# Two of the four pairs of row tiles: weights times values as seven half-size products

## The chip, the cores and the metric

The kernel runs on one core of a Trainium2 chip. The time is device microseconds of that core for one launch; shorter is better. Several runs are taken and their median is compared. One further execution is recorded by the hardware profiler; its own time and its span are given below.

## The reference

Eight sequences (batches) of 1024 rows by 256 columns, float32, go through one block: a modulated layer norm, attention without projections (both score sides are the normed rows times a vector), a gated residual, a second modulated norm, a two-layer ReLU network of inner width 1024 with a gated residual.

```python
h = layernorm(x) * (1 + ca) + sa
scores = einsum('nsd,ntd->nst', h * w_lhs, h * w_rhs)
x = x + ga * einsum('nst,ntd->nsd', softmax(scores), h)
h = layernorm(x) * (1 + cb) + sb
x = x + gb * (relu(h @ W1 + b1) @ W2 + b2)
```

`ca`, `sa`, `ga`, `cb`, `sb`, `gb` come from a small product per sequence; the gates are kept at least 0.25 away from zero. Everything stays float32. The change concerns the second `einsum`: weights times values.

## The kernel before

A batch has 1024 rows, that is eight row tiles of 128. One pass of the main loop is called a turn here: turn `i` of batch `b` handles row tile `i` of that batch. The instructions of each engine stand in the order in which the program names them (`pin` fixes that), so every engine works through one list and an instruction that waits holds up all behind it on its engine.

In a turn the kernel computes the scores of the tile two turns ahead (`direct`, L381: only blocks on or right of the diagonal; `psc` in PSUM, copied to `sc` by ScalarE), mirrors the rest (`mirror`: VectorE transposes 32x32 blocks, DMAs issued by SyncE put them in place), takes the maximum of each row (`row_max`, L431, VectorE, tile `m`), spreads that maximum along the columns with a small transposing matmul (`max_turn`, L436, `pm`), subtracts it (`subtract`, L443, VectorE) into the transposed weights `pT` (128 keys by 8 blocks by 128 rows), and exponentiates them in place (`exponent`, L452, ScalarE).

`product` (L464) then multiplies the tile's `pT` by the batch's values `xg`: eight matmuls, one for each block of 128 keys, of 257 columns (256 values and a column of ones, whose result is the sum of the row's weights), summed in one PSUM bank `po`. `product_out` takes the reciprocal of that sum (L478), scales and adds to `x` (L480) and takes the statistics of the new row for the second norm (L227, L228), all on VectorE. `ffn_stats`, `ffn_norm` and what follows need these statistics of four row tiles.

The network of the batch half before runs in the same turns. Batch `b`'s turns 0, 1, 4 and 5 hold its first layer: `pair_products` (L579) with `pair_sums` (L613 to L622), `pair_last` (L630 and, on GpSimd, L631), `pair_relu`, and `pair_turn` (L650 to L653, GpSimd). That layer already works by seven half-size products. Turns 2 and 3, 6 and 7 hold the second layer (`y_first` and `y_second`, L657, with their sums on VectorE and the transpose `y_turn`, L714). Next to this, the next batch is loaded, normed and transposed (`prepare_...`; its transposes are L305, its sides `lT` and `rT` are written at L335 and L339). Batch 0 has no network before it, and the last batch's network runs after the loop.

From batch 1 on, `product(b, i)` and `product_out(b, i)` stand at the end of each turn; only in turns 6 and 7 of the last batch do they stand at the start. `max_turn` stands between two matmuls of a turn's network part: in turns 0, 1, 4 and 5 behind the first two products of `pair_products`, in turns 2, 3, 6 and 7 inside `y_first` and `y_second`. The row maximum of tile 6 is taken on VectorE at the end of turn 4 and is wanted on TensorE early in turn 5; that of tile 7 is taken and wanted within turn 5. PSUM banks tagged `a` (four) hold `po`, `pa`, `pb`, `pc`, `ya` to `yd` in turn. Small GpSimd additions (`later`) wait in a list that `spare` takes from at fixed places.

Of the kernel before, what the change touches and what calls it, by code (L numbers as in the profile page):

```python
# [10 lines left out]
F32 = mybir.dt.float32  # L11
AF = mybir.ActivationFunctionType
ALU = mybir.AluOpType
# [3 lines left out]
P = 128  # L17
# [5 lines left out]
def adaln_block_kernel(  # L23
# [13 lines left out]
    nc = tc.nc  # L37
    B, S, D = x.shape
    INTER = W1.shape[1]
    NT = S // P  # L40
# [184 lines left out]
    def stats(mv, t, src, name):  # L225
        st = work.tile([P, nc.vector.BN_STATS_DIM], F32, tag="st", name=f"st_{name}")
        nc.vector.bn_stats(st, src)  # L227
        nc.vector.bn_aggr(mv[:, t, :], st)  # L228
# [90 lines left out]
    def prepare_turn(b, g, vector=True):  # L319

        xg, pts = xg_t[b], []
        lT = lT_t[b, g] = two.tile([P, ND, HALF], F32, tag="lT", name=f"lT_{b}_{g}", bufs=3)
        rT = rT_t[b, g] = two.tile([P, ND, HALF], F32, tag="rT", name=f"rT_{b}_{g}", bufs=3)
        rows = lambda T, k: T[:, k, :].rearrange("p (t a v) -> p t a v", a=NV, v=V)
        for k in range(ND):
            if b > 0:
                pt = pre[b, g][:, k]
            else:
                pt = ps_t.tile([P, HALF], F32, tag="t", name=f"pth_{b}_{g}_{k}")
                for j in range(TH):  # L330
                    nc.tensor.transpose(pt[:, ts(j, P)], xg[:, g * TH + j, ts(k, P)], ident)
                pt = pt.rearrange("p (t a v) -> p t a v", a=NV, v=V)
            pts.append(pt)
            if vector:
                nc.vector.tensor_scalar(  # L335
                    rows(lT, k), pt, side_col(0, 0, k, b), side_col(0, 1, k, b),
                    ALU.mult, ALU.add,
                )
            nc.scalar.activation(  # L339
                rows(rT, k), pt, AF.Identity,  # L340
                scale=side_col(1, 0, k, b), bias=side_col(1, 1, k, b),
            )
        if not vector:
            for k in range(ND):
                nc.scalar.activation(
                    rows(lT, k), pts[k], AF.Identity,
                    scale=side_col(0, 0, k, b), bias=side_col(0, 1, k, b),
                )
# [123 lines left out]
    def product_out(b, i):  # L472
        po = po_t.pop((b, i))
        g, j = divmod(i, TH)
        if j == 0:
            mvb_t[b, g] = work.tile([P, TH, 2], F32, tag="mvb", name=f"mvb_{b}_{g}")
        rl = work.tile([P, 1], F32, tag="rl", name=f"rl_{b}_{i}")
        nc.vector.reciprocal(rl, po[:, D : D + 1])  # L478
        x2 = x_tile(b, i)
        nc.vector.scalar_tensor_tensor(x2, po[:, :D], rl, x2, ALU.mult, ALU.add)  # L480
        stats(mvb_t[b, g], j, x2, f"b{b}_{i}")


    ffn = {}
# [5 lines left out]
    def spare():  # L490
        if queue:
            queue.popleft()()
# [4 lines left out]
    def ffn_stats(b, g):  # L497
        mv = mvb_t.pop((b, g))
        ffn["r", g] = mv, rstd_of(mv, "rb", f"rb_{b}_{g}")
# [269 lines left out]

    def second_out(b, a):  # L770
        q = a % 2
        if q == 0:
            out_t["o"] = work.tile([P, 2, D], F32, tag="o", name=f"o_{b}_{a}", bufs=2)
        o = out_t["o"]
        nc.vector.tensor_tensor(o[:, q, :], out_t.pop(a)[:, :D], x_tile(b, a), ALU.add)
        if a >= NT - 2:
            nc.sync.dma_start(out=out[b, ts(a, P), :], in_=o[:, q, :])
        elif q == 1:
            nc.sync.dma_start(
                out=out[b, ds((a - 1) * P, 2 * P), :].rearrange("(q p) d -> p q d", p=P),  # L780
                in_=o,
            )
# [209 lines left out]
    def weights(b, i):  # L992
        subtract(b, i)
        exponent(b, i)
# [3 lines left out]
    for b in range(B):  # L998
        for i in range(NT):
# [25 lines left out]
            if b == 0:  # L1025
# [20 lines left out]
                    subtract(*ahead)  # L1046
                norms(b, i)
                spare()
                continue
            turn_max = (lambda: max_turn(*late)) if late else (lambda: None)  # L1050

# [4 lines left out]
            if first:  # L1056
# [10 lines left out]
                if ahead:  # L1067
                    mirror(*ahead)
                pair_last(fb, fg, c)
                if c > 0:  # L1070
                    pair_turn(c - 1)
                if i == 4 and b + 1 < B:
# [8 lines left out]
                middle(b, i)  # L1081
                pair_sums(fb, fg, c + 1)
                pair_last(fb, fg, c + 1)
                if ahead and ahead != extra:
                    row_max(*ahead)
                pair_turn(c)
# [9 lines left out]
            else:  # L1096
                half = i % TH - 2
                if i == 3 and b + 1 < B:
                    prepare_stats(b + 1, 1)
                if not ahead:  # L1100

                    product(b, i)
                    product_out(b, i)
                    if i == NT - 1:
                        ffn_stats(b, 1)
                (y_second if half else y_first)(fb, fg, turn_max)
                if ahead:
                    mirror(*ahead)
                spare()
                early(b, i)  # L1110
                if late:
                    weights(*late)
                middle(b, i)
                if i == 2 and b + 1 < B:
# [19 lines left out]
            if not first:  # L1134
                if half and b < B - 1 or i == 3:
                    y_turn(fb, fg)
                for _ in range(4 if half else 1):
                    spare()
            if first or ahead:
                product(b, i)  # L1140
                product_out(b, i)
            if (b, i) == (B - 1, TH - 1):
                ffn_stats(b, 0)
            late = ahead if ahead != extra else None
# [86 lines left out]
```

## Time and profile before

| what | value |
|---|---|
| median of 3 runs | 778.18 us (778.14 to 778.81) |
| the profiled execution: its time, its span | 778.52 us, 776.6 us |
| granted TensorE clock | 1.00 |
| TensorE matmul busy | 767.0 us, 99% of the span |
| VectorE busy | 562.9 us, 72% |
| GpSimd busy | 461.5 us, 59% |
| ScalarE busy | 342.3 us, 44% |
| matmuls of weights times values (L464) | 1024 records, 233.0 us busy |

The page lists busy time for each engine, then groups of equal instructions with their number, total busy time, mean duration in ns and the idle time of the engine ahead of them. One float32 matmul of the program shows as two matmul records. Matmuls overlap, so a mean of 380 ns for one record is its latency; the time it takes from TensorE is the distance between two starts, which the timeline gives. The span leaves out what lies around the program's first and last instruction: 778.52 less 776.6, 1.9 us.

### The profile page before, as it was taken

The numbers are of one execution on the slowest core, as the hardware profiler recorded it, in microseconds if no ns is written. First come the engines' busy times: TensorE is split into PE (matmuls) and PEld (weight loads), VectorE is DVE, ScalarE is ACT, GpSimd is POOL, SyncE is SP. The second block draws the span as 40 slices with busy tenths as digits, with TensorE's granted clock in tenths as the row PEclk, the third lists the DMA queues.
The fourth block names the chain that finished last, engine by engine and source line by source line (L and its number), as shares of the span: only waits on it lengthen the run. The fifth ranks groups of instructions, "written<-read, shape, count | busy, mean of one in ns | idle before, by whom it ended". The sixth has DMA issues, their size and how long they took to land.

```text
span 776.6 us, 10553 instructions
## 1 busy us (share of the span) xinstructions
PE 767.0 (99%) x3374; PEld 619.7 (80%) x3374; DVE 562.9 (72%) x1212; ACT 342.3 (44%) x581; POOL 461.5 (59%) x573
## 2 busy tenths in 40 slices
PE   8999999999999999999999999999999999999998
PEld 3576788878887888878887888887888878888886
DVE  6597879658796688947788667966879667583632
ACT  4454545534354355434455344543535435251511
POOL 1365675936758386664857547594575927368641
PEclk9999999999999999999999999999999999999999
DMA  5314434355344364444443544445534345142220
GB/s 191 123 38 148 119 108 127 124 146 169 113 125 136 109 174 112 143 137 118 146 125 113 151 142 135 104 152 151 155 106 127 102 122 170 38 126 81 81 82 28
DMA packets 106208, 95.14 MB, mean 123 GB/s; under 512 B 29700, under 2 KB 98848, under 8 KB 106152
## 3 DMA queue, kind: packets, MB, share of 16 engines
q1 hardware_dynamic: 98408, 85.81, 37.7%
q10 hardware_dynamic: 7744, 8.65, 3.7%
q8 instruction: 27, 0.44, 0.2%
q14 instruction: 29, 0.24, 0.1%
HBM read 50.62 MB, written 43.81 MB: 122 GB/s over the span
## 4 chain that ended last, share of the span: by engine, by line
PE 88%; DVE 5%; POOL 2%; DMA 2%; issue 1%; ACT 1%; SPq 0%; DVEq 0%; POOLq 0%; ACTq 0%
PE po L464 26%; PE psc L381 15%; PE pa L579 9%; PE pb L579 6%; PE pc L579 6%; PE yc L657 6%; PE ya L657 6%; PE yb L657 6%; PE py L762 3%; PE yd L657 3%; PE pm L436 1%; POOL f L631 1%; DVE m L431 1%; DMA x<-in_L_attn_x_dram 1%; DMA D_y<-T_y 1%
## 5 line engine op out<-in xcount | busy, mean ns | idle before, releaser
L464 PE MATMUL po<-xg,pT 128*128 128x257 f32 x1024 | 233.0, 380 | 0.0
L464 PEld LDWEIGHTS po<-xg,pT 128*128 128x128 f32 x1024 | 193.9, 190 | 27.9 <-issue 1.0
L631 POOL TENSOR_TENSOR f<-f,kept 128x512 f32<-128x512 f32 x64 | 81.3, 1271 | 122.9 <-DVE f L630 104.6
L381 PE MATMUL psc<-rT,lT 128*128 128x512 f32 (+3 forms) x384 | 134.3, 486 | 0.0
L381 PEld LDWEIGHTS psc<-rT,lT 128*128 128x128 f32 x384 | 68.7, 190 | 38.7 <-issue 26.5
L388 ACT COPY sc<-psc 128x512 f32<-128x512 f32 (+3 forms) x96 | 45.0, 475 | 108.5 <-PE psc L381 108.5
L452 ACT ACTIVATE pT<-pT 128x1024 f32<-128x1024 f32 x64 | 67.1, 1048 | 50.3 <-DVE pT L443 50.2
L443 DVE TENSOR_TENSOR pT<-sc,pm 128x1024 f32<-128x1024 f32 x64 | 77.1, 1205 | 8.0 <-PE pm L436 8.0
L431 DVE TENSOR_REDUCE m<-sc 128x1 f32<-128x1024 f32 x64 | 77.3, 1209 | 0.1
L598 ACT COPY kept<-pa 128x512 f32<-128x512 f32 x64 | 37.4, 585 | 82.2 <-PE pa L579 82.2
L640 ACT ACTIVATE f<-f 128x512 f32<-128x512 f32 x64 | 40.4, 631 | 74.3 <-POOL f L631 74.3
L567 POOL TENSOR_TENSOR hs<-hT 128x256 f32<-128x256 f32 x16 | 11.6, 728 | 97.6 <-DVE hT L558 97.6
L579 PE MATMUL pb<-hs,w1s 128*128 128x256 f32 x256 | 66.0, 380 | 0.3 <-DVE f L616 0.3
L579 PE MATMUL pc<-hT,w 128*128 128x256 f32 x256 | 65.7, 379 | 0.0
L404 DVE STREAM_TRANSPOSE Tm<-sc 128x896 f32<-128x896 f32 (+6 forms) x49 | 34.7, 708 | 34.8 <-ACT sc L388 34.1
L579 PEld LDWEIGHTS pc<-hT,w 128*128 128x128 f32 x256 | 48.6, 190 | 6.6
L495 POOL TENSOR_TENSOR x<-x,rows 128x256 f32<-128x256 f32 x64 | 45.5, 739 | 12.1 <-ACT rows L865 12.1
L579 PEld LDWEIGHTS pb<-hs,w1s 128*128 128x128 f32 x256 | 45.9, 190 | 8.2 <-DVE f L616 0.8
L657 PE MATMUL yc<-f,w2s 128*128 128x256 f32 x224 | 52.1, 379 | 0.0
L613 DVE SCALAR_TENSOR_TENSOR u<-pb,cols,kept 128x256 f32<-128x256 f32 x64 | 30.5, 477 | 28.2 <-PE pb L579 27.2
L657 PEld LDWEIGHTS yc<-f,w2s 128*128 128x128 f32 x224 | 41.5, 190 | 10.2 <-issue 2.9
L651 POOL TENSOR_TENSOR ft<-ft,f 128x256 f32<-128x256 f32 x56 | 41.6, 744 | 4.4
(135 smaller groups left out, 1397.2 us busy)
## 6 DMA issues: line engine op xcount, KB each, us to landing
D_f<-T_f SPq DMA_DIRECT2D x60, 128.0 KB, 2.3
X_f<-D_f SPq DMA_DIRECT2D x15, 512.0 KB, 3.4
D_a<-T_a SPq DMA_DIRECT2D x56, 128.0 KB, 3.1
D_y<-T_y SPq DMA_DIRECT2D x56, 128.0 KB, 2.3
Y<-D_y SPq DMA_DIRECT2D x14, 512.0 KB, 4.0
out_dram<-x SPq DMA_DIRECT2D x14, 512.0 KB, 3.2
X_a<-D_a SPq DMA_DIRECT2D x13, 512.0 KB, 3.4
x<-in_L_attn_x_dram ACTq DMA_DIRECT2D x12, 512.0 KB, 3.4
```

The source lines that it names most:

```text
L381: nc.tensor.matmul(psc[:, : hi - lo], lhsT=lT_t[b, i // TH][:, k, ts(i % TH, P)], rhs=rT_t[b, n][:, k, lo - n * HALF : HALF], start=(k == ...
L388: nc.scalar.copy(score_row(b, i)[:, lo // V : hi // V, :], psc[:, : hi - lo].rearrange("p (n v) -> p n v", v=V),)
L431: nc.vector.tensor_reduce(m, score_row(b, i), AX.XY, ALU.max)
L443: nc.vector.tensor_tensor(pT.rearrange("p j (a v) -> p j a v", v=V), score_columns(b, i), pm[:, :P].rearrange("p (j a v) -> p j a v", j=1, ...
L452: nc.scalar.activation(pT_t[b, i], pT_t[b, i], AF.Exp)
L464: nc.tensor.matmul(po[:, : D + 1], lhsT=pT[:, t, :], rhs=xg_t[b][:, t, 0 : D + 1], start=(t == 0), stop=(t == NT - 1),)
L495: queue.append(lambda: nc.gpsimd.tensor_tensor(out, in0, row, op))
L579: nc.tensor.matmul(out, lhsT=lhsT, rhs=rhs, start=True, stop=True)
L631: nc.gpsimd.tensor_tensor(f[:, c::NH, hi], f[:, c::NH, hi], kept[:, None, hi].to_broadcast([P, 2, H2]), ALU.add,)
L640: nc.scalar.activation(f[:, c, :], f[:, c, :], AF.Relu)
L651: add(ft[:, 1, c], ft[:, 0, c], f[:, c, lo], ALU.add)
L657: nc.tensor.matmul(out, lhsT=lhs(c), rhs=rhs(c), start=(c == 0), stop=(c == NH - 1))
```

## The change

Row tiles 2 and 3, and row tiles 6 and 7, of batches 1 to 7 are taken together: fourteen pairs. For a pair, the weights (256 rows by 1024 keys) are a two by two block matrix: the two row tiles, and the two halves of the keys. The values are one too: the two halves of the keys, and the two halves of the columns, the second with the column of ones. Seven products of 128 rows by 512 keys by 128 or 129 columns (four matmuls each) take the place of eight.

`pair_begin` computes two of the seven, with the weights of the first tile as they are, at the start of turn 2 or 6. `left_sums` (GpSimd, four additions of 128x512) then forms the sums of the weights, partly in place in `pT`, and needs both tiles' exponentials. `right_sums` (GpSimd) forms the four sums of the values in `tsum`, once for a batch: three at the end of the turn 7 before, one in turn 0. `pair_end` computes the other five products at the end of turn 3 or 7, in two PSUM banks. `pair_begin_sum` and `pair_out` (VectorE) add the products up into `W` in SBUF. `pair_rows` does for both tiles what `product_out` did, from `W`. It stands in turn 4 behind the second `pair_last` and ahead of `row_max`; for tiles 6 and 7, and everywhere in the last batch, right after `pair_out`. In turn 2 `subtract` and `exponent` of tile 3 move ahead of `left_sums`. `max_turn` moves into `pair_begin` in turns 2 and 6.

`lT` and `rT` have two buffers in place of three, and the last batch's output tile lies in a buffer of the network (`ft`) as one piece of eight row tiles in place of two buffers of two.

```diff
@@ -319,8 +319,8 @@
     def prepare_turn(b, g, vector=True):
         xg, pts = xg_t[b], []
-        lT = lT_t[b, g] = two.tile([P, ND, HALF], F32, tag="lT", name=f"lT_{b}_{g}", bufs=3)
-        rT = rT_t[b, g] = two.tile([P, ND, HALF], F32, tag="rT", name=f"rT_{b}_{g}", bufs=3)
+        lT = lT_t[b, g] = two.tile([P, ND, HALF], F32, tag="lT", name=f"lT_{b}_{g}", bufs=2)
+        rT = rT_t[b, g] = two.tile([P, ND, HALF], F32, tag="rT", name=f"rT_{b}_{g}", bufs=2)
         rows = lambda T, k: T[:, k, :].rearrange("p (t a v) -> p t a v", a=NV, v=V)
         for k in range(ND):
             if b > 0:
@@ -479,6 +479,110 @@
         x2 = x_tile(b, i)
         nc.vector.scalar_tensor_tensor(x2, po[:, :D], rl, x2, ALU.mult, ALU.add)
         stats(mvb_t[b, g], j, x2, f"b{b}_{i}")
+    XS = D - P + 1
+    tsum = const.tile([P, 4, TH, P + 4], F32, name="tsum")
+    nc.gpsimd.memset(tsum[:, 1, :, P : P + 1], 1.0)
+    paired = lambda b, i: b > 0 and i % TH >= 2
+    def right_sums(b, which):
+        xg = xg_t[b]
+        b11, b12 = xg[:, 0:TH, P:D], xg[:, 0:TH, 0:P]
+        b21, b22 = xg[:, TH:NT, P:D], xg[:, TH:NT, 0:P]
+        t = [tsum[:, n, :, 0:P] for n in range(4)]
+        ins = [(b12, b11), (b22, t[0]), (b22, b12), (t[1], b21)]
+        for n in which:
+            nc.gpsimd.tensor_tensor(t[n], *ins[n], ALU.subtract)
+    halves = lambda pT: (pT[:, 0:TH, :], pT[:, TH:NT, :])
+    two_t = {}
+    def pair_begin(b, i, between=None):
+        W = work.tile([P, 2, D + 4], F32, tag="W", name=f"W_{b}_{i}", bufs=1)
+        pp = ps_a.tile([P, HALF], F32, tag="a", name=f"pp_{b}_{i}")
+        one, other = halves(pT_t[b, i])
+        rows = slice(P, P + XS)
+        for out, lhs, h in (
+            (pp[:, 0:XS], one, 0), (pp[:, XS : 2 * XS], other, 1)
+        ):
+            for t in range(TH):
+                nc.tensor.matmul(
+                    out, lhsT=lhs[:, t, :], rhs=xg_t[b][:, h * TH + t, P : P + XS],
+                    start=(t == 0), stop=(t == TH - 1),
+                )
+            if between and h == 0:
+                between()
+        nc.scalar.copy(W[:, 1, rows], pp[:, 0:XS])
+        two_t[b, i] = W, pp
+    def pair_begin_sum(b, i):
+        W, pp = two_t[b, i]
+        rows = slice(P, P + XS)
+        nc.vector.tensor_tensor(W[:, 0, rows], pp[:, XS : 2 * XS], W[:, 1, rows], ALU.add)
+    def left_sums(b, i):
+        (a11, a12), (a21, a22) = halves(pT_t[b, i]), halves(pT_t[b, i + 1])
+        s1 = work.tile([P, TH, P], F32, tag="s1", name=f"s1_{b}_{i}", bufs=1)
+        add = nc.gpsimd.tensor_tensor
+        add(s1, a21, a22, ALU.add)
+        add(a21, a11, a21, ALU.subtract)
+        add(a11, s1, a11, ALU.subtract)
+        add(a12, a12, a11, ALU.subtract)
+        two_t["s1"] = s1
+    def pair_end(b, i):
+        (s2, s4), (s3, a22) = halves(pT_t.pop((b, i))), halves(pT_t.pop((b, i + 1)))
+        s1 = two_t.pop("s1")
+        pq = ps_a.tile([P, HALF], F32, tag="a", name=f"pq_{b}_{i}")
+        pr = ps_a.tile([P, HALF], F32, tag="a", name=f"pr_{b}_{i}")
+        for out, lhs, rhs in (
+            (pr[:, P : 2 * P], s1, tsum[:, 0, :, 0:P]),
+            (pr[:, 2 * P : 3 * P], s3, tsum[:, 2, :, 0:P]),
+            (pq[:, 0:XS], s2, tsum[:, 1, :, 0:XS]),
+            (pq[:, XS : XS + P], a22, tsum[:, 3, :, 0:P]),
+            (pr[:, 0:P], s4, xg_t[b][:, TH:NT, 0:P]),
+        ):
+            for t in range(TH):
+                nc.tensor.matmul(
+                    out, lhsT=lhs[:, t, :], rhs=rhs[:, t, :],
+                    start=(t == 0), stop=(t == TH - 1),
+                )
+        two_t[b, i] = two_t[b, i][0], pq, pr
+    def pair_out(b, i):
+        W, pq, pr = two_t[b, i]
+        two_t[b, i] = W
+        add = nc.vector.tensor_tensor
+        rows = slice(P, P + XS)
+        first = W[:, :, 0:P]
+        u2 = W[:, 1:2, P:D].to_broadcast([P, 2, P])
+        pair = lambda at: pr[:, at : at + 2 * P].rearrange("p (j d) -> p j d", d=P)
+        add(W[:, 1, rows], pq[:, 0:XS], W[:, 1, rows], ALU.add)
+        add(first, pair(P), u2, ALU.add)
+        add(W[:, 1, P:D], W[:, 1, 0:P], pq[:, XS : XS + P], ALU.subtract)
+        add(first, pair(0), first, ALU.add)
+    def pair_rows(b, i):
+        W = two_t.pop((b, i))
+        g, j = divmod(i, TH)
+        rl = work.tile([P, 2], F32, tag="rl2", name=f"rl_{b}_{i}", bufs=1)
+        nc.vector.reciprocal(rl, W[:, :, D])
+        for q in range(2):
+            x2 = x_tile(b, i + q)
+            nc.vector.scalar_tensor_tensor(
+                x2, W[:, q, 0:D], rl[:, q : q + 1], x2, ALU.mult, ALU.add
+            )
+            stats(mvb_t[b, g], j + q, x2, f"b{b}_{i + q}")
     ffn = {}
@@ -769,9 +873,10 @@
     def second_out(b, a):
         q = a % 2
-        if q == 0:
-            out_t["o"] = work.tile([P, 2, D], F32, tag="o", name=f"o_{b}_{a}", bufs=2)
-        o = out_t["o"]
+        if a == 0:
+            O = two.tile([P, 3, NH, H2], F32, tag="ft", name="o", bufs=1)
+            out_t["o"] = O.rearrange("p j c r -> p (j c r)").rearrange("p (a d) -> p a d", d=D)
+        o = out_t["o"][:, a - q : a - q + 2]
         nc.vector.tensor_tensor(o[:, q, :], out_t.pop(a)[:, :D], x_tile(b, a), ALU.add)
         if a >= NT - 2:
             nc.sync.dma_start(out=out[b, ts(a, P), :], in_=o[:, q, :])
@@ -1046,6 +1151,9 @@
                     subtract(*ahead)
                 norms(b, i)
                 spare()
+                if i == NT - 1:
+                    assert not queue
+                    right_sums(1, range(3))
                 continue
             turn_max = (lambda: max_turn(*late)) if late else (lambda: None)
@@ -1067,6 +1175,8 @@
                 if ahead:
                     mirror(*ahead)
                 pair_last(fb, fg, c)
+                if i == 0:
+                    right_sums(b, (3,))
                 if c > 0:
                     pair_turn(c - 1)
                 if i == 4 and b + 1 < B:
@@ -1081,6 +1191,8 @@
                 middle(b, i)
                 pair_sums(fb, fg, c + 1)
                 pair_last(fb, fg, c + 1)
+                if c == 0 and (b, i - 2) in two_t:
+                    pair_rows(b, i - 2)
                 if ahead and ahead != extra:
                     row_max(*ahead)
                 pair_turn(c)
@@ -1097,18 +1209,28 @@
                 half = i % TH - 2
                 if i == 3 and b + 1 < B:
                     prepare_stats(b + 1, 1)
-                if not ahead:
-
-                    product(b, i)
-                    product_out(b, i)
-                    if i == NT - 1:
-                        ffn_stats(b, 1)
-                (y_second if half else y_first)(fb, fg, turn_max)
+                if half == 0:
+                    pair_begin(b, i, turn_max)
+                elif not ahead:
+                    pair_end(b, i - 1)
+                    pair_out(b, i - 1)
+                    pair_rows(b, i - 1)
+                    ffn_stats(b, 1)
+                if half:
+                    y_second(fb, fg, turn_max)
+                else:
+                    y_first(fb, fg)
                 if ahead:
                     mirror(*ahead)
+                if half == 0:
+                    pair_begin_sum(b, i)
+                    if i == 2:
+                        weights(*late)
+                    left_sums(b, i)
                 spare()
                 early(b, i)
-                if late:
+                if late and i != 2:
                     weights(*late)
                 middle(b, i)
                 if i == 2 and b + 1 < B:
@@ -1136,9 +1258,17 @@
                     y_turn(fb, fg)
                 for _ in range(4 if half else 1):
                     spare()
-            if first or ahead:
+            if first:
                 product(b, i)
                 product_out(b, i)
+            elif half and ahead:
+                pair_end(b, i - 1)
+                pair_out(b, i - 1)
+                if i == NT - 1:
+                    assert not queue
+                    right_sums(b + 1, range(3))
+                if i == NT - 1 or b == B - 1:
+                    pair_rows(b, i - 1)
             if (b, i) == (B - 1, TH - 1):
                 ffn_stats(b, 0)
             late = ahead if ahead != extra else None
```

## The prediction

> **What bounds the kernel now.** I read the page first: busy times, chain of waits, costliest groups.
>
> ```profile
> PE 767.0 (99%) x3374; PEld 619.7 (80%) x3374; DVE 562.9 (72%) x1212; ACT 342.3 (44%) x581; POOL 461.5 (59%) x573
> ...
> PE 88%; DVE 5%; POOL 2%; DMA 2%; issue 1%; ACT 1%; SPq 0%; DVEq 0%; POOLq 0%; ACTq 0%
> ...
> L464 PE MATMUL po<-xg,pT 128*128 128x257 f32 x1024 | 233.0, 380 | 0.0
> ```
>
> TensorE is busy throughout and makes up 88% of the chain; the product that is changed is its largest group and never waits. So TensorE time taken out counts in full, unless something else becomes late. Whether it does is seen in TensorE's timeline (start, duration) around the end of a pair: batch 3, end of turn 3, then turn 4 and the start of turn 5.
>
> ```profile
> 305.17 3.63 PE L464 MATMUL po<-xg,pT 128*128 128x257 f32 x16
> 308.63 1.03 PE L381 MATMUL psc<-rT,lT 128*128 128x256 f32 x4
> ...
> 319.12 0.61 PE L381 MATMUL psc<-rT,lT 128*128 128x128 f32 x4
> 319.56 0.60 PE L579 MATMUL pa<-hT,w 128*128 128x256 f32 x2
> 320.00 0.59 PE L579 MATMUL pa<-hs,w 128*128 128x256 f32 x2
> 320.43 0.27 PE L436 MATMUL pm<-ident,m 128*128 128x128 f32 x1
> ```
>
> No gaps: 16 records of 257 columns take 308.63 - 305.17 = 3.46 us, 0.217 each; four of 128 columns take 319.56 - 319.12 = 0.44, so 0.111 each, each with its own weight load. The last line wants tile 6's row maximum. The busy table by stages (turns 4, 5, 6 of batch 3) shows who else is full:
>
> ```profile
> 308.63:319.12 10.49, 10.49 (x51) 9.18 (x49) 9.94 (x22) 5.29 (x9) 2.84 (x3) 1.00 0.32 74
> 319.12:329.30 10.18, 10.18 (x52) 8.93 (x50) 9.95 (x20) 5.52 (x10) 9.87 (x12) 1.00 0.66 209
> 329.30:343.11 13.81, 13.81 (x58) 10.64 (x57) 6.68 (x14) 5.97 (x11) 12.90 (x18) 1.00 0.33 104
> ```
>
> The columns are length, TensorE, weight loads, VectorE, ScalarE, GpSimd. In turns 4 and 5 VectorE has 0.55 and 0.23 us free. Its timeline in turn 4:
>
> ```profile
> 310.07 0.48 DVE L480 SCALAR_TENSOR_TENSOR x<-po,rl,x 128x256 f32<-128x256 f32 x1
> 310.59 0.43 DVE L227 BATCH_NORM_STATS2 st_b<-x 128x6 f32<-128x256 f32 x1
> 311.05 0.18 DVE L228 BATCH_NORM_AGGREGATE mvb<-st_b 128x2 f32<-128x6 f32 x1
> 311.61 0.48 DVE L613 SCALAR_TENSOR_TENSOR u<-pb,cols,kept 128x256 f32<-128x256 f32 x1 [0.38 <-PE pb L579]
> ...
> 318.05 1.21 DVE L431 TENSOR_REDUCE m<-sc 128x1 f32<-128x1024 f32 x1
> ```
>
> L613 waits for TensorE's `pb`; from there VectorE works without a pause to the row maximum, which ends at 319.26. TensorE wants it at 320.43: 1.17 us of slack. The same difference is 1.16 in batches 1 and 2; in batch 4 there is a wait already, with its cause on VectorE:
>
> ```profile
> 413.43 0.32 PE L436 MATMUL pm<-ident,m 128*128 128x128 f32 x1 [0.36 <-DVE m L431]
> ```
>
> ```profile
> 407.87 1.30 DVE L305 STREAM_TRANSPOSE T_a<-xg 128x512 f32<-128x512 f32 x2 [1.53 <-DMA D_y<-T_y]
> ```
>
> [...] the trace spaces loads beside 128-column matmuls about 0.11 us apart, though one is recorded as 190 ns. [...] the same 128x512 scaling takes 536 to 546 ns writing `hT`, 537 to 958 writing `lT`.
>
> **The change part by part.** *Products.* A pair had 2 tiles x 8 matmuls x 2 records = 32 records x 0.2168 = 6.94 us. It gets 7 x 4 x 2 = 56 records x 0.1112 = 6.23. Gain 0.71 a pair, 14 pairs: **9.9 us**. The longest 128-column run in the trace is four float32 records, where runs of 16 and 40 come. Bounds: [...] weight loads one after another at 190 ns would give 10.64 for 56, a loss of 52 us. I take the measured spacing.
>
> *GpSimd.* Per pair four additions of 128x512 at 1.27 (row L631), about 5.2 us with their dependence; per batch four more of that size, 5.1. Together 14 x 5.2 + 7 x 5.1 = 108 us, GpSimd 73% busy. Hidden? In batch 4's turn 2 GpSimd comes free at 386.6 and the sums end near 392; `pair_end` starts near 396. The bias `hs` and the power for `prepare_norm` follow in its queue; the power ends near 396.5, where it ended at 396.6. In turn 6 (batch 3) the sums run 337.7 to 343, `pair_end` is near 350. Three value sums start as `pair_end` runs, ahead of the second norm's power: that needs VectorE's statistics some 4 us later anyway. Nothing on the path, except in the last batch, where turn 7 starts with `pair_end` right after `y_first`: the third sum is about 0.3 us late. If GpSimd's cover went, each microsecond of lateness would cost up to 14.
>
> *VectorE, sums.* `pair_begin_sum` and `pair_out`: five additions of 129 to 256 columns, by row L622 (415 ns for 256) 0.3, then 0.3 + 0.45 + 0.3 + 0.4 with dependence: 1.5 at the pair's end, where `product_out` had 1.3. One `product_out` leaves turn 3. Behind `y_turn` they end about 3.2 us after `pair_end`, where L613 can start 2.98 after it (311.61 - 308.63): 0.2 late. ScalarE's added copy of 129 columns, 0.3 us, lies in its idle time.
>
> *VectorE, `pair_rows` in turn 4.* From start to start in the lines above: reciprocal 0.18; twice 0.52 (L480 to L227), 0.46 (L227 to L228), about 0.1: **2.38 us**, put between `pair_last` and the maximum of tile 6. The next `pair_rows` position, end of turn 7, has cover: in turn 0 VectorE waited 2.67 us for `pb`.
>
> So the maximum ends at 10.63 + 0.2 + 2.38 = 13.21 us after the pair's end, and about 0.06 later (batch 4: 413.37 to 413.43) TensorE goes on. It arrives after 11.80. Wait 1.47; with `pb` of the next group stalled 0.15, 1.6 for each of batches 1 to 3: 4.8. Batch 4: VectorE is later by the DMA wait, whose return I take as even: 2.1 over today. Batches 5 and 6: their maximum ends at 11.22, and I take a lateness of 0.4: 11.22 + 0.4 + 2.38 + 0.06 - 11.80 = 2.26, twice 4.5. Bounds: no lateness at all, six times 1.27 = 7.6; contention of the scaling (two SBUF inputs) with GpSimd, 0.4 each, adds 2.4. Behind `max_turn` on TensorE stands all of turn 5; tile 7's maximum then keeps 0.6 us.
>
> *The last batch.* Both `pair_rows` follow at once: 0.5 at turn 4, and the 0.3 above: 0.8.
>
> *Free edits.* `lT`, `rT` with two buffers: overwritten after `direct` of tiles 3 and 7 has passed in turns 1 and 5, no wait. `max_turn` in turns 2 and 6 comes earlier by 2.6 us, against 5.8 of slack. The output tile: VectorE there waited only for TensorE. No DMA is added.
>
> **Sum** against the profiled execution's 778.52: -9.9 + 4.8 + 2.1 + 4.5 + 0.8 = +2.3, so 780.8; on the median of 778.18 (0.34 lower), **780.5 us**.
>
> **Rivals.** *Faster: the wait stays at its floor.* Same mechanism, no lateness: [...] It decides if the waits over turns 4 and 5 stay under 1.3 us a batch on average. For it: one `product_out` less in turn 3. Against: that time is lost again behind GpSimd's power. If VectorE had slack for `pair_rows`, as at every other maximum (3 to 8 us), all would come through: 769. The 1.17 us forbid it.
> *Weight loads or issue limit long runs of narrow matmuls.* At 0.120 us a record the gain is 3.1, time 787; at 190 ns, 830. Against: loads overlap in the runs of four and in transposes.
> *GpSimd becomes the bound.* Turn 6 had it 12.90 of 13.81 busy. Half a microsecond late in each pair: 7 us, 787. Against: the slack above.
>
> **How the numbers follow.** Main case 0.6, its own range 777.5 to 783.5; floor 0.22; no wait 0.03; slow matmuls 0.08; GpSimd 0.07. A fifth of a per cent, 1.6 us, is what I take to be tellable from no change. Faster: 0.17 of the floor case and no wait, 0.2. Same: the rest of the floor and the lower third of the main case, 0.27. Slower 0.53. The range of 775.2 to 784.5 leaves out the full gain and both breakdowns, and holds floor and contention.
>
> **What would show it.** Right: 128-column records 0.111 apart within `pair_end`; in turn 5 of batches 1 to 6 `max_turn` waiting 1.3 to 3 us for the row maximum, with the sum of these waits 8 to 13 us in the list of who waited for whom; no wait for GpSimd beyond 1 us. Wrong: spacing of 0.12 or more; waits at the start of `pair_end`; or no wait at `max_turn`, which would make the time 769 to 775.

## The result and the profile after

The changed kernel takes 797.43 us (median of 4 runs, 796.4 to 798.74), against 778.47 us (778.14 to 778.81) for the kernel before on the same chip. The ratio is 1.0244, 95% interval 1.0227 to 1.0262: slower by about 19 us, where 2.3 us had been forecast. The profiled execution took 797.64 us, its span is 795.6 us, the mean granted TensorE clock 0.989, where 1.00 is full speed.

The page of the changed kernel: busy times, chain of waits, and the group of the old product. In all these lines PE is TensorE, PEld its weight loads, DVE VectorE, ACT ScalarE, POOL GpSimd. A line number is that of the kernel in question: the products of the first layer, L579 before, are L683 now, and L579 is now the reciprocal in `pair_rows`.

```profile
PE 768.7 (97%) x3710; PEld 626.9 (79%) x3710; DVE 613.4 (77%) x1268; ACT 346.8 (44%) x595; POOL 572.6 (72%) x658
...
PE 71%; DVE 17%; POOL 4%; DMA 3%; issue 2%; SPq 1%; ACT 1%; DVEq 0%; POOLq 0%
...
L464 PE MATMUL po<-xg,pT 128*128 128x257 f32 x576 | 131.6, 381 | 0.0
```

TensorE's share of the chain fell from 88% to 71%, and VectorE's rose from 5% to 17%. The old product lost 448 of its 1024 records, as the change says. TensorE's busy time did not fall, although it has less to do; the timeline shows why. Start and duration of TensorE's groups in batch 3, from the end of turn 3 into turn 5 (the bracket gives the idle time before a group, and whose instruction ended it):

```profile
309.55 1.05 PE L555 MATMUL pr<-tsum,s 128*128 128x128 f32 x8
...
313.12 1.06 PE L555 MATMUL pr<-xg,pT 128*128 128x128 f32 x8
314.02 1.03 PE L381 MATMUL psc<-rT,lT 128*128 128x256 f32 x4
...
317.13 1.10 PE L683 MATMUL pc<-hT,w 128*128 128x256 f32 x4 [0.24 <-DVE W L572]
...
328.62 0.32 PE L436 MATMUL pm<-ident,m 128*128 128x128 f32 x1 [2.16 <-DVE m L431]
...
329.65 1.91 PE L683 MATMUL pc<-hT,w 128*128 128x256 f32 x4
331.36 1.06 PE L683 MATMUL pa<-hT,w1s 128*128 128x256 f32 x2
```

The reader should see three things. First, the new products run without a hitch: 40 records from 309.55 to 314.02, 4.47 us, 0.112 each. A pair has 56 of them, 6.27 us in place of 6.94: 0.67 saved, 9.4 us over fourteen pairs. Secondly, the matmul that wants tile 6's row maximum waits: 2.16 us in brackets, 2.33 from where it could have started; no other matmul starts in that time, and `pb`, the next in TensorE's list, follows at 328.78. Thirdly, the matmuls behind that wait are slow. Four records of `pc` take 331.36 - 329.65 = 1.71 us there, and 0.86 elsewhere (320.22 to 321.08 in the same trace). Half-speed matmuls count as busy (3.40 us of the 3.40 at half clock behind this wait), which is why the busy time did not fall.

TensorE's list of who waited for whom (total us, times, longest) has two new entries at its head:

```profile
PE pm L436 <- DVE m L431: 12.9, 6, 2.2
PE pc L683 <- DVE W L572: 2.7, 6, 0.8
```

Why the maximum is later than forecast is seen on VectorE in the same batch, end of turn 4:

```profile
323.63 0.42 DVE L734 TENSOR_TENSOR f<-pa,u 128x256 f32<-128x256 f32 x1
...
324.15 1.58 DVE L582 SCALAR_TENSOR_TENSOR x<-W,rl,x 128x256 f32<-128x256 f32 x1
...
326.33 0.45 DVE L582 SCALAR_TENSOR_TENSOR x<-W,rl,x 128x256 f32<-128x256 f32 x1
...
327.38 1.19 DVE L431 TENSOR_REDUCE m<-sc 128x1 f32<-128x1024 f32 x1
```

and on GpSimd beside it:

```profile
324.19 1.27 POOL L735 TENSOR_TENSOR f<-f,kept 128x512 f32<-128x512 f32 x1 [3.16 <-DVE rl L579]
...
326.40 0.97 POOL L755 TENSOR_TENSOR ft<-ft,f 128x256 f32<-128x256 f32 x1
327.45 0.73 POOL L756 TENSOR_TENSOR ft<-ft,f 128x256 f32<-128x256 f32 x1
```

The two scalings of `pair_rows` (L582) are equal, yet the first takes 1.58 us and the second 0.45. The first starts 0.04 us before GpSimd's addition and ends 0.27 us after it. GpSimd's addition takes 1.27 us, as without a scaling beside it; L755, which starts 0.07 us behind the second scaling, takes 0.97 us where L756, with no scaling beside it, takes 0.73. For tiles 2 and 3 of the last batch, where no GpSimd instruction runs beside them, the same two scalings take 0.48 and 0.45. The meeting is built into the place: L735 adds to what L734 has just written, and `pair_rows` was put right behind L734 (the bracket names L579, the reciprocal that stands between). So it happens in every one of batches 1 to 6 (1.58 us each).

Where the first scaling meets L735, the scaling alone took longer: its 1.58 us are about the 1.27 us of the addition and a rest of 0.3. By the records VectorE started first, by 0.04 us, and still was the one held; why, they do not show. The scalings at the end of turn 7 meet the value sums and are held too, to 0.98 to 1.25 and 0.81 to 0.82 us in batches 1 to 6.

The slow matmuls show in the busy table by stages (length, TensorE, weight loads, VectorE, ScalarE, GpSimd, then the granted clock, DMA share, GB/s), here for stretches of 3.41 us of the changed kernel around the wait of batch 2 and of batch 3:

```profile
230.64:234.05 3.41, 1.69 (x10) 1.21 (x8) 3.27 (x7) 1.90 (x4) 3.25 (x4) 1.00 0.83 275
234.06:237.46 3.40, 2.92 (x14) 2.61 (x15) 3.26 (x8) 0.00 (x0) 3.18 (x4) 1.00 0.46 155
326.21:329.62 3.41, 1.25 (x7) 0.93 (x6) 3.25 (x8) 1.63 (x3) 3.25 (x5) 1.00 0.81 260
329.63:333.03 3.40, 3.40 (x9) 2.66 (x8) 3.34 (x8) 0.00 (x0) 1.67 (x2) 0.50 0.63 211
```

The granted clock is 0.50 for one such stretch behind the wait in batches 3, 4, 5 and 6, which makes eight or so matmul records 0.21 us longer each, 1.7 us a time. It stays at 1.00 behind equally long waits in batches 1 and 2 (2.28 and 2.38 us).

The account, in TensorE time over what the matmuls themselves need, from the starts in both traces:

| where | before | after | difference, us |
|---|---|---|---|
| products of fourteen pairs | | | -9.4 |
| all waits at `pm` (among them six of 2.28 to 2.38; before, one in batch 4, 0.36 in its bracket) | 1.4 | 15.1 | +13.7 |
| half clock behind four of them | 0 | 6.8 | +6.8 |
| waits at `pc` in turn 4, six of 0.40 to 0.99 | 0 | 4.1 | +4.1 |
| last batch, turns 4 to 7 | | | +1.3 |
| one wait at `pa` in batch 1, turn 1 | 0 | 1.0 | +1.0 |
| start of the program | | | +1.1 |

The sum is +18.6 us, of the 19.0 by which the spans differ. The start of the program does not belong to the change: a stretch of half clock falls there in this trace (granted clock 0.50 from 12.18 to 15.60 us) and in some of those below, and in others, as in that of the kernel before (1.00), it does not.

### The profile page after: what moved, and what is told of

Its sections match the earlier page's. It is cut to its first block, busy times and chain, and to the rows that moved or that the text cites. A ratio compares the mean times of both kernels' runs of the same rounds, so it can differ in the third digit from the quotient of the medians.

```text
span 795.6 us, 11468 instructions
## 1 busy us (share of the span) xinstructions
PE 768.7 (97%) x3710; PEld 626.9 (79%) x3710; DVE 613.4 (77%) x1268; ACT 346.8 (44%) x595; POOL 572.6 (72%) x658
## 4 chain that ended last, share of the span: by engine, by line
PE 71%; DVE 17%; POOL 4%; DMA 3%; issue 2%; SPq 1%; ACT 1%; DVEq 0%; POOLq 0%
PE psc L381 12%; PE po L464 12%; PE pa L683 7%; PE pc L683 6%; PE pb L683 5%; PE yb L761 5%; PE ya L761 5%; PE yc L761 3%; PE pp L515 3%; PE py L866 3%; PE pr L555 2%; DVE pT L443 2%; PE pq L555 2%; PE yd L761 2%; DVE m L431 2%
## 5 line engine op out<-in xcount | busy, mean ns | idle before, releaser
L735 POOL TENSOR_TENSOR f<-f,kept 128x512 f32<-128x512 f32 x64 | 82.4, 1288 | 99.5 <-DVE f L734 74.8
L464 PE MATMUL po<-xg,pT 128*128 128x257 f32 x576 | 131.6, 381 | 0.0
L464 PEld LDWEIGHTS po<-xg,pT 128*128 128x128 f32 x576 | 108.9, 190 | 15.8 <-issue 1.0
L683 PE MATMUL pc<-hT,w 128*128 128x256 f32 x256 | 69.7, 397 | 2.7 <-DVE W L572 2.7
L683 PE MATMUL pb<-hs,w1s 128*128 128x256 f32 x256 | 68.5, 392 | 0.9 <-DVE f L720 0.9
L683 PEld LDWEIGHTS pc<-hT,w 128*128 128x128 f32 x256 | 50.4, 199 | 12.1 <-ACT kept L702 4.9
L599 POOL TENSOR_TENSOR x<-x,rows 128x256 f32<-128x256 f32 x64 | 45.4, 738 | 13.7 <-ACT rows L970 13.7
L683 PEld LDWEIGHTS pb<-hs,w1s 128*128 128x128 f32 x256 | 47.0, 195 | 9.0 <-DVE f L720 1.9
L755 POOL TENSOR_TENSOR ft<-ft,f 128x256 f32<-128x256 f32 x56 | 42.3, 756 | 4.4
L756 POOL TENSOR_TENSOR ft<-ft,f 128x256 f32<-128x256 f32 x56 | 40.8, 728 | 4.4
L599 POOL TENSOR_TENSOR xg<-xg,rows 128x256 f32<-128x256 f32 x56 | 42.3, 781 | 0.0
```

What stands on the lines that cost most here:

```text
L464: nc.tensor.matmul(po[:, : D + 1], lhsT=pT[:, t, :], rhs=xg_t[b][:, t, 0 : D + 1], start=(t == 0), stop=(t == NT - 1),)
L599: queue.append(lambda: nc.gpsimd.tensor_tensor(out, in0, row, op))
L683: nc.tensor.matmul(out, lhsT=lhsT, rhs=rhs, start=True, stop=True)
L735: nc.gpsimd.tensor_tensor(f[:, c::NH, hi], f[:, c::NH, hi], kept[:, None, hi].to_broadcast([P, 2, H2]), ALU.add,)
L755: add(ft[:, 1, c], ft[:, 0, c], f[:, c, lo], ALU.add)
L756: add(ft[:, 2, c], ft[:, 1, c], f[:, c + NH, lo], ALU.subtract)
```

## Experiments

Theory A: the products gain what they should, and all is lost again at hand-overs from VectorE to TensorE that `pair_rows` and `pair_out` make late; the scaling held by GpSimd and the clock that falls behind the wait make the loss larger than forecast. The rivals vary: that the clock falls for another reason than the idle time (B), that VectorE is simply full (C), that the added work costs wherever it stands or that a wait only moves elsewhere (D), that the clock falls behind any long wait (E). All runs have the kernel before beside them on the same chip; its median was 778.54 us (777.56 to 780.1) for the first four and 778.37 us (777.84 to 780.34) for the last four.

### pair_rows in turn 5

```diff
-                if c == 0 and (b, i - 2) in two_t:
-                    pair_rows(b, i - 2)
                 if ahead and ahead != extra:
                     row_max(*ahead)
...
         if i == (5 if b > 0 else 4):
+            if (b, 2) in two_t:
+                pair_rows(b, 2)
             ffn_stats(b, 0)
```

> pair_rows of tiles 2 and 3 moved from turn 4 (ahead of tile 6's row maximum) to the middle of turn 5, just ahead of ffn_stats; nothing else. Theory A (the maximum is held up by pair_rows, and the idle time so made lowers TensorE's clock): the six waits of 2.3 us before the spreading matmul of tile 6 go (14 us) and with them the stretches at half clock (7 us); 776 to 778 us. Rival B (the clock falls for another reason, such as the long runs of narrow matmuls): waits go, half clock stays, 783 us. Rival C (VectorE as a whole is too full, the delay only moves on to tile 7's maximum or the first layer): 785 us or more.

Measured: 774.91 us (774.39 to 776.98), ratio to the kernel before 0.9957, interval 0.9943 to 0.9972. One moved call takes 22.5 us off the changed kernel and makes it faster than the kernel before. TensorE's timeline at the same place, turn 5 of batch 3:

```profile
321.09 0.27 PE L436 MATMUL pm<-ident,m 128*128 128x128 f32 x1
321.20 1.03 PE L683 MATMUL pb<-hs,w1s 128*128 128x256 f32 x4
```

No wait, and no slow matmul: the records of `pb` and `pc` take 381 ns in the mean, 392 and 397 in the changed kernel, and there is no stretch of half clock between the start and the end of the program. So rival B falls: the long runs of narrow matmuls are all still there. The products keep their gain, and both the waits at `pm` and the clock hang on where `pair_rows` stands. VectorE comes to the call at 330.76, when TensorE is already in turn 6. Its first scaling is held by GpSimd there too (0.86 us in three batches, 1.55 in the other three), but the waits at `pm` are gone.

### One SBUF input in the scaling

The scalings of `pair_rows` in turn 4 read a PSUM tile in place of `x`, so the residual of tiles 2 and 3 is left out in batches 1 to 6; their size and the order of the instructions stay.

```diff
...
+            if i == 2 and b < B - 1:
+                other = pm_t[b, 5][:, :P].rearrange("p (j d) -> p j d", j=1)
+                nc.vector.scalar_tensor_tensor(
+                    x2.rearrange("p (j d) -> p j d", d=P),
+                    W[:, q, 0:D].rearrange("p (j d) -> p j d", d=P),
+                    rl[:, q : q + 1],
+                    other.to_broadcast([P, 2, P]),
+                    ALU.mult,
+                    ALU.add,
+                )
+            else:
...
```

> In pair_rows of turn 4 the two scalings read a PSUM tile (the spread maximum of tile 5) in place of x: one SBUF input in place of two, same size; the residual of tiles 2 and 3 of batches 1 to 6 is left out so. Theory A (the first scaling takes 1.58 us because two SBUF inputs meet GpSimd's addition): it takes 0.48, each wait for tile 6's maximum falls from 2.3 to 1.2 us, 6.6 us less, and if the shorter gap keeps the clock up 7 us more: 784 to 791. Rival (the scaling is slow because of W itself or a wait that the profile does not name): 1.5 us as before, 797.

Measured: 784.72 us (783.23 to 787.38), ratio 1.0081, interval 1.0055 to 1.0106. The first scaling in VectorE's timeline of batch 3:

```profile
321.67 0.48 DVE L585 SCALAR_TENSOR_TENSOR x<-W,rl,pm 128x256 f32<-128x256 f32 x1
```

and GpSimd's addition beside it, from GpSimd's timeline:

```profile
321.71 1.27 POOL L747 TENSOR_TENSOR f<-f,kept 128x512 f32<-128x512 f32 x1 [3.12 <-DVE rl L580]
```

The scaling starts again 0.04 us before the same addition. It now takes 0.48 us, and GpSimd's next two additions take 0.73 each. In all six batches the twelve scalings take 0.45 to 0.48. So the second SBUF input made the difference: beside the same addition the scaling took 1.58 us with it and 0.48 without. The waits at `pm` shrink to 1.15 to 1.26 us from start to start, and no clock falls behind them (records of `pc` take 381 ns in the mean, 397 in the changed kernel). TensorE's list of waits:

```profile
PE pm L436 <- DVE m L431: 6.2, 6, 1.1
```

The meeting with GpSimd costs 12.7 us (797.43 less 784.72) in all: some 6.7 in the six waits (15.1 to 8.4 us at `pm`), and the rest, about 6, is put down to the clock.

### Only tiles 6 and 7 as pairs

Tiles 2 and 3 go by the old `product` and `product_out`.

```diff
-                if half == 0:
+                if i < TH:
+                    pass
+                elif half == 0:
                     pair_begin(b, i, turn_max)
...
-                    y_first(fb, fg)
+                    y_first(fb, fg, turn_max if i < TH else None)
...
-            if first:
+            if first or i < TH:
                 product(b, i)
                 product_out(b, i)
```

> Only tiles 6 and 7 are taken as pairs (7 pairs, not 14); tiles 2 and 3 use the old product. Theory A (the loss is all in turns 4 and 5 behind the pair of tiles 2 and 3): half of TensorE's gain, 4.7 us, less about 1 us in the last batch: 774 to 776 us, no half clock. Rival D (the added GpSimd and VectorE work costs wherever it stands): 783 or more, with waits in turns 0 and 1 too.

Measured: 774.49 us (773.99 to 775.45), ratio 0.9947, interval 0.993 to 0.9964; neither new wait is in TensorE's list. Half of the pairs should save 7 x 0.67 = 4.7 us, and the spans differ by 776.6 - 772.2 = 4.4. So the seven pairs whose `pair_rows` stands at the end of turn 7 cost next to nothing, and the loss is that of tiles 2 and 3 alone. Rival D falls here, although the scalings in turn 7 are held by GpSimd as well.

### The wait filled with matmuls

```diff
         pm = ps_t.tile([P, HALF], F32, tag="t", name=f"pm_{b}_{i}")
+        if i == 6 and 0 < b < B - 1:
+            for _ in range(5):
+                nc.tensor.matmul(
+                    pm[:, 0:D], lhsT=ident, rhs=xg_t[b][:, 0, 0:D], start=True, stop=True
+                )
```

> The changed kernel with five matmuls of 256 columns (2.16 us on TensorE, result overwritten) ahead of the spreading matmul of tile 6 in batches 1 to 6, where TensorE otherwise idles 2.3 us. Theory A (idling lowers the clock): VectorE's lateness stays, filler and rest of the wait add up to 2.3 us as before, but no stretch at half clock follows: 7 us less, 790 to 791. Rival B: half clock stays, 797 or a little more.

Measured: 793.66 us (791.39 to 793.85), ratio 1.0185, interval 1.0165 to 1.0206; 790 to 791 had been expected. TensorE's list of waits has one of the six left:

```profile
PE pm L441 <- DVE m L431: 2.0, 1, 2.0
```

In five of the six batches there is neither that wait nor a fall of the clock. In batch 3 the maximum was later still, because VectorE had waited for a DMA in turn 4, and the filler left a wait of 2.0 us; behind that one the clock fell (four records of `pb` take 1.23 us from start to start there, 0.86 elsewhere). VectorE's timeline there:

```profile
320.53 1.30 DVE L305 STREAM_TRANSPOSE T_a<-xg 128x512 f32<-128x512 f32 x2 [2.04 <-DMA D_y<-T_y]
```

The filler takes as long as the waits did (five times 0.43, 2.16 us). The 3.8 us by which the time still drops against 797.43 are put down to the falls that stay out, three of four (some 5 us), less batch 3's longer wait. Rival B falls again: VectorE is as late as before, and in the five batches where TensorE had work in the meantime the clock stayed up (0.997 in the mean of the whole run, 0.989 in the changed kernel). So the clock is a cost of its own, beside the wait.

### The wanting matmul later

```diff
-                pair_products(fb, fg, c, turn_max)
+                hold = i == 5 and b < B - 1
+                pair_products(fb, fg, c, None if hold else turn_max)
...
                 pair_last(fb, fg, c)
+                if hold:
+                    turn_max()
```

> pair_rows stays in turn 4 and meets the same GpSimd work; only the small matmul that wants tile 6's row maximum is moved on TensorE, from behind two products of turn 5's first group to behind the whole group. Theory A (one late hand-over, VectorE has room after it): no wait for the maximum, no half clock behind it, the scaling still takes 1.58 us in the trace, time as with pair_rows moved away, 775 to 778 us. Rival C (VectorE is the limit of turns 4 and 5 together, so what it is late must be paid at the next hand-over): the wait comes back at pb, pa or pc of turn 5, some 1.5 to 2.3 us in each of six batches, time 783 to 790 us.

Measured: 796.45 us (794.44 to 797.73), ratio 1.0225, interval 1.0207 to 1.0244: no better than the changed kernel. Theory A fell here, and rival C held, though dearer than priced. TensorE in turn 5 of batch 3:

```profile
328.05 0.67 PE L683 MATMUL pa<-hT,w 128*128 128x256 f32 x2 [0.36 <-DVE x L480]
...
329.75 0.32 PE L436 MATMUL pm<-ident,m 128*128 128x128 f32 x1 [0.60 <-DVE m L431]
330.66 2.07 PE L683 MATMUL pb<-hs,w1s 128*128 128x256 f32 x4 [0.59 <-DVE f L720]
332.53 1.78 PE L683 MATMUL pc<-hT,w 128*128 128x256 f32 x4
```

The wait for tile 6's maximum is gone, but what VectorE is late is paid at the next three hand-overs: for the bank of `pa`, for tile 7's maximum, for the bank of `pb`. From start to start these are 0.58, 0.77 and 0.80 us over what the matmuls need, 2.1 together. Behind them the clock falls all the same (the last line, 1.78 us for four records), in batches 3, 5 and 6. The table by stages says why there was no room: turns 4, 5 and 6 of batch 3 of this kernel.

```profile
312.55:323.76 11.21, 10.72 (x51) 9.10 (x50) 10.90 (x24) 5.74 (x10) 3.66 (x4) 1.00 0.32 73
323.76:338.05 14.29, 12.74 (x52) 10.10 (x50) 13.41 (x26) 6.53 (x12) 12.23 (x14) 0.88 0.46 147
338.05:351.00 12.95, 12.95 (x60) 9.95 (x59) 7.09 (x13) 5.55 (x11) 12.40 (x15) 1.00 0.39 113
```

VectorE (the third pair of numbers after the length) is busy 10.90 of 11.21 us in turn 4 and 13.41 of 14.29 in turn 5. In the first experiment, whose `pair_rows` it reaches only in turn 6, it is busy 10.68 of 10.95 and 9.43 of 10.18 there, so it has 1.0 us for the 3.4 that `pair_rows` takes with the held scaling. Only turn 6 has room, 5.9 us in the table. So theory A is mended: it is not one hand-over that is late, but VectorE that has no room for `pair_rows` before turn 6, whichever instruction of TensorE comes to want it.

### pq in another bank

As the first experiment, and besides:

```diff
-        pq = ps_a.tile([P, HALF], F32, tag="a", name=f"pq_{b}_{i}")
+        pq = ps_t.tile([P, HALF], F32, tag="t", name=f"pq_{b}_{i}")
```

> pair_rows in turn 5 as in e1, and besides pq in a PSUM bank of the other set (that of the transposes and row maxima), so that pc of turn 4 need not wait until pair_out has read pq. Theory A: the wait at pc, 4.1 us in all in e1, is gone, and nothing else waits for the bank: 770.5 to 772 us. Rival D (the bank is wanted by the transposes and row maxima as well, and the wait only moves there): 774 to 776 us, with waits at pm or at the transposes of turn 4 behind pair_out.

Measured: 771.87 us (771.47 to 772.82), ratio 0.9914, interval 0.99 to 0.9928. The six waits at `pc` are gone; in their place stands one of 0.5 us in the list, at `pa` in batch 4. TensorE in turn 4 of batch 3:

```profile
307.94 1.03 PE L683 MATMUL pb<-hs,w1s 128*128 128x256 f32 x4
308.81 1.03 PE L683 MATMUL pc<-hT,w 128*128 128x256 f32 x4
```

Start to start, `pb` to `pc` is 0.87 us here and 1.27 in the changed kernel. 3.0 us are gained on the first experiment, of the 4.1 that the waits at `pc` took. Rival D falls, but for that one wait. `pc` of turn 4 had waited for the bank of `pq`, which `pair_out` empties only behind `y_turn` and its own first additions.

### The last batch by the old product for tiles 2 and 3

As the experiment before, and besides:

```diff
+                single = b == B - 1 and i < TH
...
-            if first:
+            if first or single:
                 product(b, i)
                 product_out(b, i)
```

> As e6, and in the last batch tiles 2 and 3 go by the old product, so that nothing of the pair stands ahead of the hand-overs of the last turns 4 and 5. Theory A: the waits of the last batch's turns 4 and 5 (some 1.5 us) go, against 0.67 us of gain given up: 0.5 to 1 us below e6. Rival (these waits come from the end of the kernel, which the old product has too): 0.5 to 0.7 us above e6.

Measured: 771.64 us (770.43 to 773.03), ratio 0.9911, interval 0.9897 to 0.9926. The spans say what was expected, 769.1 against 769.6: waits of 1.3 us go, 0.67 of gain is given up. The times overlap with those of the experiment before and do not tell the two apart.

### Half a clock stretch later

Four added matmuls of 256 columns, ahead of the spreading matmul of tile 4 in turn 2 of batch 4, put all that follows 1.74 us later, about half of the 3.41 us that a fall lasts. In the changed kernel the falls begin at 12.18, 329.62, 425.20, 520.77 and 616.34 us, that is 317.44 and three times 95.57 us apart, close to 93 and 28 times 3.41. The question is whether it matters where a wait lies in steps of 3.41 us counted from the falls.

```diff
         pm = ps_t.tile([P, HALF], F32, tag="t", name=f"pm_{b}_{i}")
+        if (b, i) == (4, 4):
+            for _ in range(4):
+                nc.tensor.matmul(
+                    pm[:, 0:D], lhsT=ident, rhs=xg_t[b][:, 0, 0:D], start=True, stop=True
+                )
```

> The changed kernel with four matmuls of 256 columns (eight records, 1.74 us) added once, in turn 2 of batch 4, where TensorE is never waited for; all waits stay as they are, [...]. Theory A [...]: in batch 4 [...] the fall behind it stays out (1.7 us saved), and in batches 5 and 6 [...] they fall again; total within 0.5 us of the changed kernel. Rival E (any gap of 2.3 us is followed by a fall from batch 3 on, wherever it lies): falls in batches 3 to 6 as before, total 1.7 us over the changed kernel. [...]

Measured: 796.22 us (one run), the six waits as before (13.0 us in the list, longest 2.2). The falls lie behind batches 2, 3 and 6, not 3 to 6. The table by stages for the two stretches around the wait of batch 4:

```profile
424.34:427.75 3.41, 2.12 (x11) 1.89 (x12) 3.31 (x7) 0.82 (x2) 3.33 (x5) 1.00 0.42 125
427.76:431.16 3.40, 3.40 (x17) 2.88 (x16) 3.36 (x8) 0.59 (x1) 1.65 (x2) 1.00 0.63 218
```

Rival E falls: in batch 4 a wait of 2.30 us is followed by full clock, and in batch 2 one brings a fall that it did not bring in the changed kernel. Theory A's word on batch 4 held; that batches 5 and 6 would both fall did not: behind that of batch 5, where no step of the table below holds over 1.70 us, the clock stayed at 1.00. The total says little, since this run also lacked the half-clock stretch at the start (mean clock 0.993, 0.989 in the changed kernel). For three kernels TensorE's idle time was summed in steps of 3.41 us, counted from the falls of the same run. Idle is here what lies between one record's start, plus the time that its width takes in a run without gaps (0.11 us for 128 columns, 0.216 for 256), and the next start. For each batch the step with the most idle time:

| kernel | batch 1 | 2 | 3 | 4 | 5 | 6 |
|---|---|---|---|---|---|---|
| changed | 1.88 | 1.88 | **2.38** | **2.36** | **2.36** | **2.36** |
| wanting matmul later | 1.74 | 1.40 | **2.33** | 1.34 | **2.23** | **2.24** |
| half a stretch later | 1.38 | **2.34** | **2.33** | 1.34 | 1.70 | **2.35** |

Bold is followed by a fall. Every step here with 2.23 us or more is, none with 1.88 or less is; the one fall of the filler kernel follows 2.20. The point between was not looked for. The order holds by starts only: by the busy time of the table by stages, in which the modelled end of the last matmul before each gap counts as busy, batch 3 of the middle row is idle 1.52 us and falls, and batch 1 of the changed kernel is idle 1.83 and does not. In the middle row the fall of batch 3 follows three short waits, of 0.58, 0.77 and 0.80 us, and not one long one.

## Why the prediction was wrong

The direction was right, the size was not: the forecast was 780.5 us, at most 784.5.

*Products.* Right. 112 ns a record in runs of up to 40, against 111.2 taken; 9.4 us gained, against 9.9. The rival of slow narrow matmuls is excluded.

*GpSimd hidden.* Right as to TensorE's own waits for it, 0.2 us in all, in the last batch; the rival in which GpSimd becomes the bound by its own lateness is out, too. Wrong in one place, through VectorE. The step let three value sums stand ahead of the second norm's power, since that needed VectorE's statistics some 4 us later anyway. At the end of batch 0 GpSimd comes to them late: they run from 84.00 to 87.85 us, the power (L233) ends at 88.83, and VectorE stands 2.73 us for it, where it stood for nothing before. From there VectorE works without a pause to 96.69, and TensorE's `pa` in turn 1 has waited 1.0 us by then, released by VectorE's statistics L227. The two traces lead there; no run tests it. What the step also did not see is that GpSimd's work can slow VectorE's while both count as busy, so that neither shows a wait (1.58 us in place of 0.48 for the first scaling of `pair_rows`, with no idle time in its line).

*pair_rows in turn 4.* The mechanism was right: `max_turn` waits in turn 5 of batches 1 to 6, in all 12.9 us in the list, within the 8 to 13 named. The size agrees by luck only. Without the meeting the six waits are 1.15 to 1.26 us, near the floor of 1.27; the 2.1 and 2.26 of batches 4 to 6, put there for lateness, are not seen in any batch. In their place all six carry 1.1 us of a held scaling: in batch 3 `pair_rows` takes 3.42 us (323.96 to 327.38), where 2.38 had been taken (its parts, as written, add up to 2.34). The prediction had named that contention and priced it at 0.4 each, an estimate from the span of 537 to 958 ns of another operation; it measured 1.1. It could have been read from the code: L735 starts as L734 ends (0.14 us behind it in batch 3), and `pair_rows` stands right behind.

*What stands behind the wait.* This is the step that failed by omission: the sum prices each wait at its length, and puts at nothing what the wait does to the matmuls behind it. Behind four of the six waits of 2.28 to 2.38 us in this trace the clock was at half for 3.41 us, which cost 1.7 us more each: 6.8 us. The granted clock of 1.00 in all stages of the kernel before showed no such thing; the longest wait in its list is 1.4 us. The least idle time that a fall followed in these runs is 2.20 us within 3.41.

*VectorE, sums.* The step followed the additions of `pair_out` to L613 (0.2 us late) and missed who wants the bank that they read: `pc` waits for `pq`'s, 0.4 to 1.0 us a batch, 4.1 in all. This is the second term put at nothing. The bank experiment showed it.

*The last batch.* 0.8 forecast, 1.3 found. *Free edits.* None of them waits.

*The sum.* By the account above, what belongs to the change came to 17.5 us (18.6 less the start of the program) in place of 2.3. Of the 15.2 between them 6.8 are the clock, 4.1 the bank of `pq`, 2.3 the longer waits at `pm`, 1.0 the value sums in batch 1, and 0.5 each the products and the last batch. The clock is the largest, but not enough by itself: without it the time would be 790.6 us by this account, still above 784.5.

*The floor rival* (776.4 us: 778.18 less 9.9, with 7.6 for the waits and 0.5 for the last batch) is what the second experiment came nearest to, without reaching it: its waits are at the floor, but `pc` adds 4.3 us, smaller waits add the rest, and it stays at 784.72. The rival in which all of the gain comes through needed VectorE to have room. It has, though not in turn 4: with `pair_rows` reached in turn 6 and `pq` in another bank, 771.87 us were reached, 6.5 below the kernel before.

## What to carry to other kernels

Work that is moved onto an engine has to be placed by that engine's free time stage by stage, and where the stage is full, moving the consumer instead of the work only moves the wait: here one call put 12 us later on VectorE made 22.5 us of difference. Beside the queue, ask of each inserted VectorE instruction with two SBUF inputs what GpSimd runs at that very moment, above all the GpSimd instruction that the VectorE instruction just ahead sets free: here that made 1.58 us of 0.48. Price a TensorE wait of two microseconds not at its length alone, but with the clock that it may lose (here 1.7 us behind four of six waits), and count waits that lie close together as one (here three of 0.58 to 0.80 us were followed by a fall).

## What the runs showed of the hardware

- A VectorE scaling of 128x256 float32 with two SBUF inputs took 1.58 us when a GpSimd addition of 128x512 (1.27 us) started 0.04 us after it, in six of six batches, and 0.45 to 0.48 with no GpSimd instruction beside it; with one input in PSUM it took 0.45 to 0.48 beside the same addition. Where GpSimd started second by 0.07 us against the second scaling, it was GpSimd's addition of 128x256 that took 0.97 us in place of 0.73.
- In batches 1 to 6 of these runs the granted TensorE clock was 0.50 for 3.41 us behind each step of 3.41 us, counted from the falls, that held 2.20 us or more of idle time by starts; behind steps with 1.88 us or less it stayed at 1.00. Six waits of 2.28 to 2.38 us were followed by four such falls in the changed kernel, and six of about that length by three in the kernel half a stretch later.
- Float32 matmul records of 128 columns, each with its own weights, kept 112 ns from start to start over 40 records.
